# Causal attention with a mixture of experts: row maxima by one masked reduction for each query block and head

## The chip, the cores and the metric

The kernel runs on one core of a Trainium2 chip. The core has five engines that run their own instruction streams and wait for one another by semaphores: TensorE (PE in the profile; its weight loads are listed as PEld), VectorE (DVE), ScalarE (ACT), GpSimd (POOL) and SyncE (SP), which issues transfers. The metric is the time of one execution on the device in microseconds. The kernel before takes 564.23 us, the median of three runs (562.38, 564.23, 564.98).

## The reference

The input x has 8 batches of 512 tokens with 128 features. The result is x plus a causal attention of 16 heads of 8 dimensions and plus a mixture of 8 experts (two for each token, by a softmax over router logits) with one shared expert; both work on the layer-normalised x. Cut to the part that the change touches:

```python
h = jnp.swapaxes((xn @ W1 + b1).reshape(B, S, H, 3 * d), 1, 2)   # H = 16, d = 8, S = 512
q, k, v = h[..., :d], h[..., d:2*d], h[..., 2*d:]
w = jnp.einsum('bhqd,bhkd->bhqk', q, k) / d ** 0.5
mask = jnp.tril(jnp.ones((S, S)))
w = jax.nn.softmax(w * mask - (1.0 - mask) * 1e6, axis=-1)       # causal
a = jnp.einsum('bhqk,bhkd->bhqd', w, v)
...
x + a.reshape(B, S, E) @ Wp + bp + moe(xn)
```

The softmax needs, for each query and head, the largest score over the keys up to the query itself.

## The kernel before

**Tiling.** A batch has four blocks of 128 queries (NC = 4, P = 128). Four heads form a group, so that there are 32 groups (8 batches, 4 groups each), and the loop at line 1219 goes over them. A group's work is cut into five steps (TILES, line 329), 160 steps in all. Two things happen with the scores. The transposed scores (keys on the partitions; tile scT, function fill) go through the exponential on ScalarE (weigh, L465, tile pT) and then into the products with v (attend, L489). Before that the maximum of each query's row has to be known, so the scores are computed a first time with the queries on the partitions (tile sc, function peak_scores) only to take their maxima (function maxima). This runs AHEAD = 9 steps before the exponential of the same scores. At the end of a group, shift_parts turns the maxima of the four heads into two parts, shift transposes them (mT) and put_shift stores them by two small transfers into two extra rows of the queries, so that the later product scT subtracts the maxima by itself.

**Which maxima come from which tile.** Every sc tile has 128 partitions, two heads (index t) and 512 columns of f32, and there is one such buffer (pool m_ps). Of a group's five steps, steps 0 and 2 (MASKED_TILES) hold the four diagonal blocks of two heads each: eight products of 128 columns. Steps 1 and 3 hold, for two heads each, query block 3 with the keys of blocks 0 to 2 (384 columns) and query block 1 with the keys of block 0 (128 columns). Step 4 holds query block 2 with the keys of blocks 0 and 1 for all four heads. Query block 0 has nothing below its diagonal block.

**Masking.** Only diagonal blocks need the mask. In most of the kernel the mask lies in sc before the products are added to it: prepare (called at line 1236, one step ahead) lets ScalarE copy mask_q into the buffer (L371), and the products accumulate onto it (start is false). While the routing still runs, prepare is not called; there peak_scores puts the mask on by four products of an identity with mask_q2 (mask_half, L324).

**Maxima.** Diagonal tiles are reduced into diag by one reduction of 1024 elements (L417), steps 1 and 3 into tops by two reductions (768 elements, L421, and 256, L422), step 4 by one of 1024 (L412). shift_parts first combines tops and diag by a maximum (L427). tops is set to a very small number once (L194), so that block 0, for which nothing is written there, takes its maximum from diag.

**What sets the order.** The order on TensorE, VectorE, ScalarE and SyncE is the program's order, written out by hand (line 87); each engine takes its instructions one after the other, and one that waits holds up all behind it. A step (lines 1222 to 1254) issues, in this order: fill and the exponential (weigh); the sc products and the maxima of nine steps later (look); one piece of the experts' work (extra): products gu (L651), a tanh on ScalarE (L656), two VectorE instructions th and h (L657, L659); then shift_parts, prepare, a piece of the routing, up to two entries of side (mostly the products y, L682), and what was put off (attend, evacuate, divide, turn, join). Products gu, y and most small ones share three buffers of the pool mi_ps. The routing runs on VectorE until it is done, in the first 140 us or so, and prepare and the routed experts start after it.

Of the kernel before, what the change touches and what calls it, by code (L numbers as in the profile page):

```python
# [10 lines left out]
F32 = mybir.dt.float32  # L11
I32 = mybir.dt.int32
BF16 = mybir.dt.bfloat16
F32R = mybir.dt.float32r
AF = mybir.ActivationFunctionType
ALU = mybir.AluOpType
AX = mybir.AxisListType
# [8 lines left out]
P = 128  # L26
B, S, E = 8, 512, 128
H, D = 16, 8
NC = S // P
# [6 lines left out]
AHEAD = 9  # L36
# [22 lines left out]
MASKED = -1e30  # L59
WHOLE = 1.5 * 2.0**23  # L60
LEAST = -3e38
QK = 4 * D
SIDE = 64
# [4 lines left out]
def attn_moe_kernel(  # L68
# [14 lines left out]
    nc = tc.nc  # L83
    const = ctx.enter_context(tc.tile_pool(name="const", bufs=1))
# [43 lines left out]
    for i in range(NV):  # L128
        t = const.tile([P, NC, H, 32], F32, name=f"v_ext{i}")
# [11 lines left out]
    def constant_rows(t, rows):  # L141
# [4 lines left out]
                fills[:rows].unsqueeze(1).to_broadcast([rows, NU * HP * NC, P]),  # L146
            )

    mask_q = const.tile([P, P], BF16, name="mask_q")
    nc.gpsimd.memset(mask_q, 0.0)  # L150
    nc.gpsimd.affine_select(
        out=mask_q, in_=mask_q, pattern=[[-1, P]], compare_op=ALU.is_ge, fill=MASKED,
        base=0, channel_multiplier=1,
    )
    eye_2 = const.tile([P, 2, P], BF16, name="eye_2")
    mask_q2 = const.tile([P, 2, P], BF16, name="mask_q2")
    mask_k2 = const.tile([P, 2, P], BF16, name="mask_k2")
    for m, sign, compare, fill in (
        (mask_q2, 1, ALU.is_ge, MASKED), (mask_k2, -1, ALU.is_ge, MASKED),
        (eye_2, 1, ALU.not_equal, 1.0),  # L160
    ):
        nc.gpsimd.memset(m, 0.0)
        for t in range(2):
            nc.gpsimd.affine_select(
                out=m[ts(t, SIDE)], in_=m[ts(t, SIDE)], pattern=[[sign * SIDE, 2], [-sign, P]],
                compare_op=compare, fill=fill, base=0, channel_multiplier=sign,
            )
    for t in v_ext:
# [9 lines left out]
        out=before, in_=before, pattern=[[1, P]], compare_op=ALU.is_gt, fill=-1.0,  # L178
        base=0, channel_multiplier=-1,
# [7 lines left out]
        out=upto, in_=upto, pattern=[[1, NE], [-1, NE]], compare_op=ALU.is_ge, fill=0.0,  # L187
        base=0, channel_multiplier=0,
# [2 lines left out]


    tops = const.tile([P, 2, 2, NC], F32, name="tops")
    nc.vector.memset(tops, LEAST)  # L194
    diag = const.tile([P, 2, 2, NC], F32, name="diag")

    xnT = const.tile([E, NT * P], F32, name="xnT")

# [2 lines left out]
    for i in range(2):  # L201
        t = const.tile([P, NF, PAIR], F32, name=f"h{i}")
# [6 lines left out]
        own_p, pattern=[[0, 1]], base=0, channel_multiplier=1, allow_small_or_imprecise_dtypes=True  # L209
# [3 lines left out]
        upto_p, pattern=[[1, P]], base=0, channel_multiplier=0, allow_small_or_imprecise_dtypes=True  # L213
# [14 lines left out]
    at = pool("at", 2)  # L228
# [5 lines left out]
    m_ps = pool("m_ps", 1, space=PSUM)  # L234
# [82 lines left out]
    def rows_of(n, jj, rows):  # L317
        u, i, t = n // 2 % NU, n % 2 * 2 + jj // 2, jj % 2
        at_ = slice(SIDE * t, SIDE * t + rows)
        return qs[at_, u, i, :], ks[at_, u, i, :]  # L320

    def mask_half(out_, t, k, mask):

        nc.tensor.matmul(  # L324
            out_, lhsT=eye_2[ts(t, SIDE), k], rhs=mask, start=False, stop=True,
            skip_group_check=True,
        )

    TILES = [("wide", 0), ("wide", 2), ("mixed", 0), ("mixed", 2), ("half", 0)]
    NTILES = len(TILES)  # L330
# [30 lines left out]

    MASKED_TILES = (0, 2)
    ahead = []

    def prepare(n, i):

        ps = m_ps.tile([P, 2, S], F32, name="sc")
        if i in MASKED_TILES:  # L370
            nc.scalar.copy(  # L371
                ps.rearrange("p t (b k) -> p (t b) k", k=P),
                mask_q.unsqueeze(1).to_broadcast([P, 2 * NC, P]),
            )
        ahead.append(ps)

    def peak_scores(n, i):
        ready_ = bool(ahead)
        ps = ahead.pop() if ready_ else m_ps.tile([P, 2, S], F32, name="sc")

        def part(at_, jj, c, key, count, start):
            q, k = rows_of(n, jj, QK + 1 if n else QK)
            nc.tensor.matmul(  # L383
                ps[:, jj % 2, ts(at_, P) if count == 1 else ds(at_ * P, count * P)],
                lhsT=q[:, ts(c, P)], rhs=k[:, key * P : (key + count) * P],
                start=start, stop=True, skip_group_check=True,
            )

        j = i // 2 * 2
        if i == 4:  # L390
            blocks = [(0, 0, 2, 0, 2, True), (2, 2, 2, 0, 2, False)]
        elif i in MASKED_TILES:
            blocks = [(c, j, c, c, 1, not ready_ and c == 0) for c in range(NC)]
        else:
            blocks = [(0, j, 3, 0, 3, True), (3, j, 1, 0, 1, False)]
        for at_, jj, *rest in blocks:
            for t in range(2):
                part(at_, jj + t, *rest)
        if i in MASKED_TILES and not ready_:
            for k in range(2):  # L400
                for t in range(2):
                    mask_half(
                        ps[:, t].rearrange("p (b k) -> p b k", k=P), t, k,
                        mask_q2[ts(t, SIDE), k].unsqueeze(1).to_broadcast([SIDE, NC, P]),
                    )
        return ps

    def maxima(n, i):

        ps = peak_scores(n, i)  # L410
        if i == 4:
            nc.vector.tensor_reduce(  # L412
                tops[:, :, :, 2],
                ps.rearrange("p t (u k) -> p t u k", u=2), AX.X, ALU.max,
            )
        elif i in MASKED_TILES:
            nc.vector.tensor_reduce(  # L417
                diag[:, :, i // 2, :], ps.rearrange("p t (b k) -> p t b k", k=P), AX.X, ALU.max
            )
        else:  # L420
            nc.vector.tensor_reduce(tops[:, :, i // 2, 3], ps[:, :, : 3 * P], AX.X, ALU.max)  # L421
            nc.vector.tensor_reduce(tops[:, :, i // 2, 1], ps[:, :, 3 * P :], AX.X, ALU.max)  # L422

    def shift_parts(n):

        top = at.tile([P, 2, 2 * NC], F32, name="row_max")
        nc.vector.tensor_tensor(  # L427
            top.rearrange("p t (i c) -> p t i c", c=NC), tops, diag, ALU.max
        )
        parts = at.tile([P, 2, 2, 2 * NC], F32R, name="m_parts")  # L430
        hi, lo = parts[:, :, 0], parts[:, :, 1]
        nc.vector.tensor_scalar_mul(hi, top, -1.0)
        nc.vector.scalar_tensor_tensor(lo, top, -1.0, hi.bitcast(F32), ALU.mult, ALU.subtract)
        return parts
# [298 lines left out]
    total_steps = B * NG * NTILES  # L733
# [48 lines left out]
    count = ro.tile([P, PURE + 2 * MIXED], F32, name="count")  # L782
# [368 lines left out]
    done_routing = []  # L1151
# [50 lines left out]
    for b in range(1, B):  # L1202
        at_ = 5 * NG * (b - 1)
# [15 lines left out]
    for n in range(B * NG):  # L1219
        b, g = divmod(n, NG)  # L1220
        waiting = []
        for i, (kind, j) in enumerate(TILES):
            step = n * NTILES + i
            if i == 1 and n % 2 == 1 and (n + 3) // 2 < 2 * B:
                fetch((n + 3) // 2)
            by_pool = step >= BUSY and len(placed) < NB
            spare = step >= total_steps - AHEAD + 1 and step % 2 == 1
            waiting.append((kind, j, weigh(n, kind, j, by_pool, spare)))
            while to_place:
                to_place.pop(0)()  # L1230
            parts_then = look(step + AHEAD) if step + AHEAD < total_steps else lambda: None
            if step not in alone:
                extra()
            parts_then()
            if done_routing and step + AHEAD + 1 < total_steps:
                prepare(*divmod(step + AHEAD + 1, NTILES))
            if step >= routed:
                some_routing()
            side(step, 2)
            for f in late:  # L1240
                f()
            behind(step)
            late = []
            if i == NTILES - 1 and n == B * NG - 1:
                evacuate(n, av, halves[0])
            if i == 1 and g % 2 == 0:
                av = av_ps.tile([P, S], F32, name="av")
            if i in (1, 4) or (i == 3 and n == B * NG - 1):
                late = [partial(attend, n, waiting, av)]
                waiting = []  # L1250
            if len(placed) == NB:
                for _ in range(2):
                    if to_gather and (to_gather[0][1] < kept or through):
                        gather(*to_gather.pop(0))
        if n == B * NG - 1:
            break
        if g % 2 == 1:
            late.append(partial(evacuate, n, av))
            due(step + 3, partial(divide, n))
        if g == NG - 1:  # L1260
            due(step + 4, partial(turn, b))
            due(step + 5, partial(join, b), behind_all)
# [78 lines left out]
```

## Time and profile before

| what | value |
| --- | --- |
| median of three runs | 564.23 us |
| the profiled execution's own time | 565.0 us |
| its span in the profile | 562.8 us |
| mean granted TensorE clock | 0.992 |
| instructions in the span | 12501 |
| L383, sc products: count, busy, mean | 896, 81.9 us, 282 ns |
| L324, mask products into sc from mask_q2: count, busy, mean | 56, 8.8 us, 382 ns |
| L465, exponential: count, busy, mean | 156, 159.9 us, 1025 ns |
| L657 and L659, th and h: count each, busy | 156, 64.9 us and 66.0 us |

Busy time is the union of an engine's instructions. A group's mean is of its instructions' lengths from start to end; the next instruction on the same engine may start before the end of one that it doesn't wait for. Idle time before a group is put down to whatever ended it. The span is that of the instructions in the trace; the execution's own time has a little more around it.

### The profile page before, as it was taken

Reading aid. Unit: us, or ns where it says so; the run is one execution under the profiler, and the core shown is the slowest. Engines: PE = TensorE matmul, PEld = TensorE weight load, DVE = VectorE, ACT = ScalarE, POOL = GpSimd, SP = SyncE. Lnnn points to the kernel's source line nnn. Section 1 sums busy time; section 2 is a strip of 40 time slices with the busy share of each in tenths; the row PEclk is TensorE's granted clock in tenths of the full one; section 3 lists DMA queues with packets and bytes.
Section 4 is the critical chain, followed back from the end, with each engine's and each line's share of the span. In section 5 each row is a group of like instructions: output and inputs, shape, how many; then the busy total and the mean of one; then the engine's idle time right before and its main releaser. Section 6 shows DMA issues by size and latency. Waiting matters only on the chain.

```text
span 562.8 us, 12501 instructions
## 1 busy us (share of the span) xinstructions
PE 530.4 (94%) x4495; PEld 381.8 (68%) x4495; DVE 435.0 (77%) x1057; ACT 354.6 (63%) x567; POOL 261.8 (47%) x442
## 2 busy tenths in 40 slices
PE   4899988889999999999999999999999999989994
PEld 3676655557675777777776777667776777768762
DVE  5878998999877877777786887777787877877731
ACT  4453444463566866777677776677677767766553
POOL 8630020001342656666556656656555755543730
PEclk9999998899999999999999999999999999999999
DMA  7651362616228495685829584775928596750694
GB/s 217 146 75 19 77 116 58 96 59 122 65 64 142 131 154 147 118 204 115 156 72 160 176 137 124 129 168 134 175 84 152 154 155 185 147 135 4 103 255 95
DMA packets 34114, 70.72 MB, mean 126 GB/s; under 512 B 7028, under 2 KB 9336, under 8 KB 34054
## 3 DMA queue, kind: packets, MB, share of 16 engines
q1 hardware_dynamic: 26278, 56.47, 45.7%
q0 software_dynamic: 6912, 13.20, 12.3%
q8 instruction: 36, 0.59, 0.5%
q10 hardware_dynamic: 864, 0.27, 0.2%
q14 instruction: 24, 0.20, 0.2%
HBM read 52.38 MB, written 17.33 MB: 124 GB/s over the span
## 4 chain that ended last, share of the span: by engine, by line
PE 76%; DVE 18%; DMA 2%; ACT 2%; issue 2%; SPq 0%; DVEq 0%; ACTq 0%
PE gu L651 25%; PE av L489 12%; PE y L682 11%; PE scT L339 9%; PE sc L383 9%; DVE diag L417 3%; PE qk_ps L264 3%; DVE there L1065 2%; DMA qs<-mT 2%; DVE tops L421 2%; DVE h L659 1%; DVE th L657 1%; PE s_ps L627 1%; PE p_ps L577 1%; PE ot L540 1%
## 5 line engine op out<-in xcount | busy, mean ns | idle before, releaser
L465 ACT ACTIVATE pT<-scT 128x1024 f32<-128x1024 f32 x156 | 159.9, 1025 | 66.3 <-PE scT L339 28.3
L472 POOL TENSOR_SCALAR_AFFINE_SELECT pT<-pT 128x256 f32<-128x256 f32 (+1 forms) x174 | 73.7, 437 | 186.5 <-ACT pT L465 182.8
L651 PE MATMUL gu<-sT,w 128*128 128x256 f32 (+1 forms) x480 | 122.5, 382 | 0.3 <-DVE h L659 0.3
L417 DVE TENSOR_REDUCE diag<-sc 128x8 f32<-128x1024 f32 x64 | 78.2, 1221 | 45.1 <-PE sc L383 32.4
L656 ACT ACTIVATE th<-gu 128x256 f32<-128x256 f32 x156 | 59.8, 383 | 65.5 <-PE gu L651 61.0
L383 PE MATMUL sc<-ks,qs 33*128 33x128 f32 (+3 forms) x896 | 81.9, 282 | 9.9 <-DVE tops L422 4.2
L651 PEld LDWEIGHTS gu<-sT,w 128*128 128x128 f32 x480 | 76.6, 189 | 17.2 <-DVE h L659 0.5
L489 PE MATMUL av<-pT,v_ext 128*32 128x512 f32 (+3 forms) x1024 | 82.9, 441 | 1.8 <-ACT pT L465 1.3
L657 DVE SCALAR_TENSOR_TENSOR th<-th,gu 128x256 f32<-128x256 f32 x156 | 64.9, 416 | 23.2 <-ACT th L656 19.0
L339 PE MATMUL scT<-qs,ks 35*128 35x512 f32 (+3 forms) x498 | 78.6, 372 | 3.5 <-DMA qs<-mT 2.3
L666 POOL DMA_INDIRECT results<-o,goal x72 | 73.2, 1016 | 16.2 <-issue 16.2
L613 POOL DMA_INDIRECT s<-table,token x72 | 69.9, 971 | 21.0 <-issue 16.7
L339 PEld LDWEIGHTS scT<-qs,ks 35*128 35x128 f32 x498 | 39.6, 184 | 58.7 <-issue 24.9
L383 PEld LDWEIGHTS sc<-ks,qs 33*128 33x128 f32 (+1 forms) x896 | 66.9, 187 | 17.8 <-DVE diag L417 4.9
L659 DVE TENSOR_TENSOR h<-gu,th 128x256 f32<-128x256 f32 x156 | 66.0, 423 | 5.4
L421 DVE TENSOR_REDUCE tops<-sc 128x2 f32<-128x768 f32 x64 | 60.8, 950 | 1.8 <-PE scT L339 0.5
L682 PE MATMUL y<-w,h 128*128 128x128 f32 x432 | 60.0, 275 | 0.7 <-DVE parts L266 0.7
L682 PEld LDWEIGHTS y<-w,h 128*128 128x128 f32 x432 | 57.2, 191 | 4.6 <-DVE parts L266 1.1
L371 ACT CAST sc<-mask_q 128x1024 f32<-128x1024 bf16 x50 | 51.0, 1020 | 6.1 <-DVE tops L422 4.5
L651 PE MATMUL gu<-xnT,ws_sb 128*128 128x256 f32 x192 | 54.1, 408 | 0.0
L489 PEld LDWEIGHTS av<-pT,v_ext 128*32 128x32 f32 x1024 | 25.4, 109 | 24.0 <-issue 14.4
L412 DVE TENSOR_REDUCE tops<-sc 128x4 f32<-128x1024 f32 x32 | 39.0, 1220 | 2.3 <-PE sc L383 2.0
(209 smaller groups left out, 577.5 us busy)
## 6 DMA issues: line engine op xcount, KB each, us to landing
w<-in_w_exp_dram SPq DMA_DIRECT2D x40, 576.0 KB
ks<-dk SPq DMA_DIRECT2D x60, 128.0 KB
dq<-parts SPq DMA_DIRECT2D x16, 256.0 KB
dk<-parts SPq DMA_DIRECT2D x16, 256.0 KB
qs<-dq SPq DMA_DIRECT2D x64, 64.0 KB
x_sb<-results POOLq DMA_DIRECT2D x16, 256.0 KB
qs<-dq SPq DMA_DIRECT2D x30, 128.0 KB
table<-rows SPq DMA_DIRECT2D x4, 520.0 KB
```

The source lines that it names most:

```text
L339: nc.tensor.matmul(out_, lhsT=k[:, ts(i, P)], rhs=q[:, i * P :], start=first, stop=True, skip_group_check=True,)
L383: nc.tensor.matmul(ps[:, jj % 2, ts(at_, P) if count == 1 else ds(at_ * P, count * P)], lhsT=q[:, ts(c, P)], rhs=k[:, key * P : (key + cou ...
L417: nc.vector.tensor_reduce(diag[:, :, i // 2, :], ps.rearrange("p t (b k) -> p t b k", k=P), AX.X, ALU.max)
L421: nc.vector.tensor_reduce(tops[:, :, i // 2, 3], ps[:, :, : 3 * P], AX.X, ALU.max)
L465: nc.scalar.activation(pT, ps, AF.Exp, scale=D**-0.5)
L472: m = nc.gpsimd.affine_select(out=d, in_=d, pattern=[[0, d.shape[1]], [1, P]], compare_op=ALU.is_ge, fill=0.0, base=0, channel_multiplier=-1,)
L489: nc.tensor.matmul(av[32 * jj : 32 * jj + 32, c * P :], lhsT=v_ext[b % NV][:, c, at_, :], rhs=weights, start=(c == 0 and g % 2 == 0), stop ...
L651: nc.tensor.matmul(gu[:, i, part], lhsT=w[c][:, ds(i * FP + f * P, P)], rhs=sT[:, part], start=True, stop=True,)
L657: nc.vector.scalar_tensor_tensor(th, th, 1.0, gu[:, 0], ALU.add, ALU.mult)
L659: nc.vector.tensor_tensor(h[own_, f], gu[own_, 1], th[own_], ALU.mult)
L666: d = nc.gpsimd.indirect_dma_start(results, bass.IndirectOffsetOnAxis(ap=goal[:, at_ : at_ + 1], axis=0), o, None, bounds_check=PLACES - 1 ...
L682: nc.tensor.matmul(y, lhsT=h[:, f, ts(c, P)], rhs=w[c % len(w)][:, ds(2 * FP + f * P, P)], start=(f == 0), stop=(f == NF - 1),)
```

## The change

The scores of a query block and head are no longer split into a diagonal block and the rest. One product covers all keys up to and with the block's own, and one VectorE instruction adds a mask to it and takes the maximum along the row. Steps 0 and 2 of a group now hold query block 3 of two heads (512 columns each), steps 1 and 3 blocks 2 and 0 (384 and 128 columns each), and step 4 block 1 of all four heads (256 columns each). The number of columns in a group stays what it was, 5120; the products of a group become 16 instead of 28. The mask is a strip of 512 columns, until, made once on GpSimd: zero, but MASKED above the diagonal in the last 128 columns. A block of c + 1 key blocks uses its last (c + 1) x 128 columns. The instruction writes the masked scores back to their place in sc and the maximum to one column of tops. With it go prepare and the copies of the mask, the mask products into sc, mask_q and mask_q2, diag, the first setting of tops, and the maximum that combined tops and diag.

```diff
-    mask_q = const.tile([P, P], BF16, name="mask_q")
-    nc.gpsimd.memset(mask_q, 0.0)
-    nc.gpsimd.affine_select(
-        out=mask_q, in_=mask_q, pattern=[[-1, P]], compare_op=ALU.is_ge, fill=MASKED,
-        base=0, channel_multiplier=1,
-    )
...
-    mask_q2 = const.tile([P, 2, P], BF16, name="mask_q2")
     mask_k2 = const.tile([P, 2, P], BF16, name="mask_k2")
     for m, sign, compare, fill in (
-        (mask_q2, 1, ALU.is_ge, MASKED), (mask_k2, -1, ALU.is_ge, MASKED),
+        (mask_k2, -1, ALU.is_ge, MASKED),
         (eye_2, 1, ALU.not_equal, 1.0),
     ):
...
     tops = const.tile([P, 2, 2, NC], F32, name="tops")
-    nc.vector.memset(tops, LEAST)
-    diag = const.tile([P, 2, 2, NC], F32, name="diag")
+    until = const.tile([P, S], BF16, name="until")
+    nc.gpsimd.memset(until, 0.0)
+    nc.gpsimd.affine_select(
+        out=until, in_=until, pattern=[[-1, S]], compare_op=ALU.is_ge, fill=MASKED,
+        base=S - P, channel_multiplier=1,
+    )
...
-    def prepare(n, i):
-        ps = m_ps.tile([P, 2, S], F32, name="sc")
-        if i in MASKED_TILES:
-            nc.scalar.copy(
-                ps.rearrange("p t (b k) -> p (t b) k", k=P),
-                mask_q.unsqueeze(1).to_broadcast([P, 2 * NC, P]),
-            )
-        ahead.append(ps)
...
     def peak_scores(n, i):
-        ready_ = bool(ahead)
-        ps = ahead.pop() if ready_ else m_ps.tile([P, 2, S], F32, name="sc")
...
+        ps = m_ps.tile([P, 2, S], F32, name="sc")
         j = i // 2 * 2
         if i == 4:
-            blocks = [(0, 0, 2, 0, 2, True), (2, 2, 2, 0, 2, False)]
-        elif i in MASKED_TILES:
-            blocks = [(c, j, c, c, 1, not ready_ and c == 0) for c in range(NC)]
+            blocks = [(0, 0, 1), (2, 2, 1)]
+        elif i % 2 == 0:
+            blocks = [(0, j, 3)]
         else:
-            blocks = [(0, j, 3, 0, 3, True), (3, j, 1, 0, 1, False)]
-        for at_, jj, *rest in blocks:
+            blocks = [(0, j, 2), (3, j, 0)]
+        for at_, jj, c in blocks:
             for t in range(2):
-                part(at_, jj + t, *rest)
...
+                q, k = rows_of(n, jj + t, QK + 1 if n else QK)
+                nc.tensor.matmul(
+                    ps[:, t, ds(at_ * P, (c + 1) * P)], lhsT=q[:, ts(c, P)],
+                    rhs=k[:, : (c + 1) * P], start=(at_ == 0), stop=True,
+                    skip_group_check=True,
+                )
+        return ps, blocks

     def maxima(n, i):
-        ps = peak_scores(n, i)
...
+        ps, blocks = peak_scores(n, i)
+        for at_, jj, c in blocks:
+            for t in range(2):
+                cols = slice(at_ * P, (at_ + c + 1) * P)
+                nc.vector.tensor_tensor_reduce(
+                    ps[:, t, cols], ps[:, t, cols], until[:, S - (c + 1) * P :], 1.0, LEAST,
+                    ALU.add, ALU.max, tops[:, t, jj // 2, c : c + 1],
+                )

     def shift_parts(n):
-        top = at.tile([P, 2, 2 * NC], F32, name="row_max")
-        nc.vector.tensor_tensor(
-            top.rearrange("p t (i c) -> p t i c", c=NC), tops, diag, ALU.max
-        )
+        top = tops.rearrange("p t i c -> p t (i c)")
...
             parts_then()
-            if done_routing and step + AHEAD + 1 < total_steps:
-                prepare(*divmod(step + AHEAD + 1, NTILES))
```

## The prediction

> **What bounds the kernel now.** I read first the busy times and the chain of waits, to see which engine sets the end; then busy time by stage; then the groups of instructions with shapes kept apart, for prices; then the timeline, for the distance from one start to the next. The page first (busy time, then the chain by engine):
>
> ```profile
> PE 530.4 (94%) x4495; PEld 381.8 (68%) x4495; DVE 435.0 (77%) x1057; ACT 354.6 (63%) x567; POOL 261.8 (47%) x442
> ...
> PE 76%; DVE 18%; DMA 2%; ACT 2%; issue 2%; SPq 0%; DVEq 0%; ACTq 0%
> ```
>
> TensorE (PE) holds the chain, but VectorE (DVE) owns 18% of it, and ScalarE (ACT), from which the change takes its copies, only 2%. By stage (busy us of each engine, instructions in brackets, then granted clock and DMA share):
>
> ```profile
> 0.00:26.00 26.00, 17.32 (x74) 12.55 (x74) 18.99 (x77) 12.23 (x25) 19.66 (x78) 1.00 0.69 191
> 26.00:142.00 116.00, 106.46 (x943) 70.60 (x945) 104.81 (x286) 55.32 (x86) 13.67 (x37) 0.97 0.40 77
> 142.00:535.00 393.00, 386.88 (x3260) 286.47 (x3253) 303.98 (x674) 274.55 (x441) 223.16 (x323) 1.00 0.63 132
> 535.00:562.80 27.80, 19.73 (x225) 12.14 (x225) 7.19 (x23) 12.47 (x17) 5.34 (x7) 0.96 0.77 175
> ...
> 60.00:140.00 80.00, 71.60 (x701) 46.61 (x697) 75.64 (x220) 39.08 (x53) 5.72 (x11) 0.96 0.44 92
> ```
>
> So there are two regimes. While the routing runs (26 to 142 us) VectorE is nearly full: 75.64 of 80 us, 94.6%, in its densest part, beside a PE at 89.5%. After it (142 to 535) PE is full, 386.88 of 393, 98.4%, and VectorE has 89 us to spare. No peak score (sc) is written before 26 or after 535, so the change acts on the two middle stages. They hold 7 and 25 of the 32 four-head groups, as L412, which runs once per group, starts at 39.0, 55.0, 72.0, 85.5, 104.7, 123.9, 142.3 and so on.
>
> Prices (group, shapes, count | busy, mean ns of one | idle before it, and its releaser):
>
> ```profile
> L417 DVE TENSOR_REDUCE diag<-sc 128x8 f32<-128x1024 f32 x64 | 78.2, 1221 | 45.1 <-PE sc L383 32.4 <-PE sc L324 4.5 <-PE gu L651 4.4
> L421 DVE TENSOR_REDUCE tops<-sc 128x2 f32<-128x768 f32 x64 | 60.8, 950 | 1.8 <-PE scT L339 0.5 <-PE sc L383 0.5
> L412 DVE TENSOR_REDUCE tops<-sc 128x4 f32<-128x1024 f32 x32 | 39.0, 1220 | 2.3 <-PE sc L383 2.0
> L422 DVE TENSOR_REDUCE tops<-sc 128x2 f32<-128x256 f32 x64 | 26.4, 412 | 0.0
> L371 ACT CAST sc<-mask_q 128x1024 f32<-128x1024 bf16 x50 | 51.0, 1020 | 6.1 <-DVE tops L422 4.5 <-DVE tops L412 1.3
> ```
>
> Between 950 and 412 ns lie 512 elements: 1.05 ns per element, and some 145 ns that each instruction pays anyway. The timeline (start, length) tells how much of that is hidden:
>
> ```profile
> 264.19 0.15 DVE L639 TENSOR_TENSOR w_own<-s,second 128x4 f32<-128x4 f32 x1
> 264.38 0.16 DVE L641 TENSOR_TENSOR scale<-w_own 128x2 f32<-128x2 f32 x1
> 264.48 0.96 DVE L421 TENSOR_REDUCE tops<-sc 128x2 f32<-128x768 f32 x1
> 265.35 0.42 DVE L422 TENSOR_REDUCE tops<-sc 128x2 f32<-128x256 f32 x1
> 265.95 0.42 DVE L657 SCALAR_TENSOR_TENSOR th<-th,gu 128x256 f32<-128x256 f32 x1 [0.18 <-ACT th L656]
> 266.40 0.42 DVE L659 TENSOR_TENSOR h<-gu,th 96x256 f32<-96x256 f32 x1
> ```
>
> L422 needs nothing of L421 and starts 0.87 us after it, 0.80 for 768 elements and 0.07. L659 waits for L657's result and starts 0.45 after it, 0.267 for 256 elements and 0.187. The tiny L641 waits for L639 and starts 0.19 after it; L421, which doesn't wait, starts 0.10 after L641 (0.078 at the median of such pairs). So an instruction costs its elements plus 0.07 us where the next is free, plus 0.187 us where the next waits for its end.
>
> **Removed on VectorE.** Each row counted until the next one starts, the means are 1.189 (L417), 0.869 (L421), 0.369 (L422), 1.214 (L412) and 0.166 us (L427, the combining maximum). A group has 2, 2, 2, 1 and 1 of them: 6.23 us.
>
> **Added on VectorE.** A group gets 16 masked reductions: four each of 512, 384, 128 and 256 elements, 5120 as before, 5.33 us at 1.04 ns. In the changed program's instruction list each is a main instruction and a read-out of one element per partition into tops, and every main one after the first of its tile waits on VectorE's own semaphore. Neither has a row here. From below: the next main cannot start before this one has ended, 187 ns a pair over its elements. From above: the read-out waits for the drained main and the next main for the read-out, twice 187, 374 ns. I take the read-out as following free (65 ns) and then costing what the tiny L639 costs a waiter (187): 252 ns, since a one-element write is nearest to that row. A group is then 5.33 + 16 x 0.252 = 9.37 us, or +3.13 (8.33, +2.1, at the low end; 11.32, +5.1, at the high one). Queued behind these waits are th and h (L657, L659); for h wait the y products (L682) and, over the three "mi" buffers, the next gu (L651); for the maxima waits the next sc product, as sc has one buffer.
>
> A rule of the Trainium skill bears on this: VectorE: DVE Perf Modes, section "The DRAIN you can't avoid", has the next op start only when the pipe is empty. The starts of L421 and L422 (0.87 apart, row 0.96) disagree. By the rule whole rows would count on both sides, 5.33 + 16 x (0.145 + 0.151) = 10.07 against 6.55 us for a group, +3.5 instead of +3.13, some 13 us more in the end. The same page, section "Two Vector instructions with no wait between them", counts an op with an accumulator output as two instructions; no run here shows one yet.
>
> **Removed on PE.** From first sc product to the next other product a diagonal tile takes 0.54 us (eight of 128 columns); two products of 512 columns are priced by scT, 0.34:
>
> ```profile
> 260.99 0.61 PE L383 MATMUL sc<-ks,qs 33*128 33x128 f32 x8
> 261.53 1.13 PE L651 MATMUL gu<-sT,w 128*128 128x256 f32 x4
> ...
> 266.54 0.50 PE L339 MATMUL scT<-qs,ks 35*128 35x512 f32 x2
> 266.88 0.41 PE L383 MATMUL sc<-ks,qs 33*128 33x256 f32 x4
> ```
>
> The other tiles keep four products each. That is 0.2 us x 50 tiles = 9.9 us off PE after 142 us. Before it, 14 diagonal tiles with four mask products each (L324, 56 x 382 ns) shrink from 1.04 to 0.34 us, 9.8 us; I count nothing for these, as VectorE decides there (were it not full, PE would hand back up to 9.8).
>
> **Removed on ScalarE, moved, and at no cost.** The 50 copies (51 us) go; ScalarE is 63% busy and 2% of the chain, so I count 0, bounded by a gain of 2%, 11 us. They also held sc for 1.02 us between VectorE's last read and PE's next product; now VectorE alone releases it. No DMA is moved. GpSimd's mask building trades rows of 0.20 + 0.28 + 0.30 + 0.85 us for a memset and a select over 512 columns (L472 takes 0.62 for that many), hidden as its setup ends near 13.5 us and the first sc product starts at 26.1; uncovered it would be 1 us at most.
>
> **The sum.** Early stage: (104.81 + 7 x 3.13) / 0.946 = 133.9 us against 116, +17.9. Late stage: PE would need (386.88 - 9.9) / 0.984 = 383.1; VectorE needs (303.98 + 25 x 3.13) / 0.946 = 404.1 and is the bound, against 393, +11.1. Together +29.0. The profiled run took 565.0 (span 562.8 and 2.2 around it), 0.8 over the median of 564.2, which the three runs' spread covers; on the median I forecast 593.
>
> **Rivals.** (1) *The read-out hides*, 187 to 220 ns a pair. For it: a one-element instruction can be as short as 78 ns to a free follower. At 187 the early stage gives +10.3; VectorE's late need, 376.9, falls below PE's 383.1, -9.9: 564.6. At 220 it is 576. (2) *Faster*: the pair's wait is no wait for the end, so a pair costs 65 + 78 = 143 ns, +1.39 a group. Early +5.1, late -9.9 since PE's shorter diagonal tiles decide: 559.4. It decides below 184 ns, where both stages cancel; against it stands the semaphore wait in the instruction list. (3) *The read-out is serialized*, 374 ns: early +32.4, late (303.98 + 127) / 0.946 = 455.6, +62.6: 659. For it: L659 and L641 show that a dependent start costs 187 every time. (4) *Lockstep*: with PE at 93% (377.0 of 404.1 us) and VectorE at 95%, and one sc buffer between them, neither reaches 94.6%; at the 90.4% of the whole early stage the same work gives 140.2 and 422.9 us, +54: 618. Against it: 60 to 140 us held 94.6% beside a PE at 89.5%.
>
> **Chances and range.** Forecast, pair at 220 to 300 ns (576 to 619): 0.50. Rival 1: 0.15. Rival 2: 0.09. Rivals 3 and 4, above 619: 0.26. A change of under 0.5% (561.4 to 567.0) can't be told from none here. Rival 2 gives faster 0.08; rivals 1 and 2 around zero, same 0.07; the rest slower, 0.85. From 568 to 640 I leave out about 2 in 10: rival 2 with half of rival 1 below, the full price of rival 3 above.
>
> **What would show it.** Right: VectorE above 500 us busy and over 90% between the stages, its share of the chain above half; starts of successive mains of 256 elements about 0.52 us apart; PE idle before sc, released by VectorE; ScalarE near 304 us. Wrong: a pair under 0.46 us at 256 elements with PE still above 97% late (rivals 1, 2), above 0.6 us (3), or VectorE below 92% with PE below 92% (4). An element rate other than 1.04 ns in the main instruction would break the sum at its first term.

## The result and the profile after

The changed kernel takes 582.89 us (median of four runs, 581.5 to 584.8) against 563.31 us for the kernel before beside it: a ratio of 1.032, 95% interval 1.027 to 1.037. It is slower by 19.6 us. The profiled run took 582.0 us with a span of 580.1.

The page of the changed kernel, busy times and the chain by engine:

```profile
PE 535.5 (92%) x4055; PEld 364.8 (63%) x4055; DVE 498.1 (86%) x1824; ACT 309.4 (53%) x517; POOL 261.7 (45%) x439
...
PE 63%; DVE 29%; issue 4%; ACT 2%; POOL 1%; DMA 0%; DVEq 0%; ACTq 0%; POOLq 0%
```

VectorE is busy for 63 us more and its part of the chain grows from 18% to 29%; TensorE keeps the larger part. ScalarE lost 45 us of work, and nothing is to be seen of it in the time. Busy time by stage, in the same columns as before (PE, PEld, DVE, ACT, POOL, granted clock, DMA). The bounds are the same events as 142 and 535 before: the first reduction of step 4 in group 6 and in group 31, now near 157 and 553:

```profile
26.00:157.00 131.00, 113.23 (x814) 72.70 (x816) 120.31 (x449) 55.50 (x86) 14.06 (x38) 0.86 0.36 70
157.00:553.00 396.00, 386.18 (x2957) 268.66 (x2950) 351.53 (x1274) 229.82 (x390) 223.14 (x322) 1.00 0.61 131
```

The stage of the routing grew by 15 us (116 to 131) and the long stage after it by 3 (393 to 396). In the first, VectorE's busy time grew by 15.5 us, as much as the stage itself, and its idle time stayed where it was (11.2 us before, 10.7 now): there VectorE's new work and the added time are of one size. (That is not a rule for the stage: e7_split_inner below adds 7.7 us there and pays 2.) In the second VectorE got 47.5 us more to do and the time hardly moved. The 3 us by themselves are not more than profiles differ: by the same events this stage took 391.5, 395.8 and 396.6 us in three later runs with the same late groups (e5, e11, e12), 390.7 in e2_late_only, and 388.6 in e3_early_only, whose late groups are those of the kernel before. The medians of e2_late_only say it better. PE's granted clock in the routing stage fell from 0.97 to 0.86, a point that comes back below.

The groups with their shapes kept apart (count | busy, mean ns | idle before, releasers), the four lengths of the masked reduction and the read-out:

```profile
L386 DVE CUSTOM_DVE_ANT_0 sc<-sc,until 128x512 f32<-128x512 f32 x128 | 89.2, 697 | 17.3 <-PE sc L373 11.9 <-PE gu L615 1.2 <-POOL rstd L798 0.6
L386 DVE DVE_READ_ACCUMULATOR2_ANT tops<- 128x1 f32 x512 | 71.9, 140 | 0.0
L386 DVE CUSTOM_DVE_ANT_0 sc<-sc,until 128x384 f32<-128x384 f32 x128 | 71.7, 560 | 4.0 <-PE sc L373 0.9 <-issue 0.3
...
L386 DVE CUSTOM_DVE_ANT_0 sc<-sc,until 128x256 f32<-128x256 f32 x128 | 55.0, 430 | 5.5 <-PE sc L373 1.2 <-PE s_ps L591 1.1
...
L386 DVE CUSTOM_DVE_ANT_0 sc<-sc,until 128x128 f32<-128x128 f32 x128 | 38.3, 299 | 4.4
```

The timeline of VectorE over one tile of steps 1 and 3 (start, length) shows what a pair costs:

```profile
274.66 0.54 DVE L386 CUSTOM_DVE_ANT_0 sc<-sc,until 128x384 f32<-128x384 f32 x1
275.14 0.13 DVE L386 DVE_READ_ACCUMULATOR2_ANT tops<- 128x1 f32 x1
275.30 0.57 DVE L386 CUSTOM_DVE_ANT_0 sc<-sc,until 128x384 f32<-128x384 f32 x1
275.78 0.14 DVE L386 DVE_READ_ACCUMULATOR2_ANT tops<- 128x1 f32 x1
275.96 0.30 DVE L386 CUSTOM_DVE_ANT_0 sc<-sc,until 128x128 f32<-128x128 f32 x1
276.18 0.14 DVE L386 DVE_READ_ACCUMULATOR2_ANT tops<- 128x1 f32 x1
276.35 0.30 DVE L386 CUSTOM_DVE_ANT_0 sc<-sc,until 128x128 f32<-128x128 f32 x1
276.57 0.14 DVE L386 DVE_READ_ACCUMULATOR2_ANT tops<- 128x1 f32 x1
276.57 0.42 DVE L621 SCALAR_TENSOR_TENSOR th<-th,gu 128x256 f32<-128x256 f32 x1
```

The read-out starts 83 ns after the main instruction's elements are through (0.48 us after the start for 384 elements, 0.22 for 128, at 1.04 ns each). The next masked reduction, which waits, starts 0.16 to 0.18 us after the read-out, 175 ns at the median of 352. But th, which waits for nothing on VectorE, starts with the read-out. So a pair costs 258 ns over its elements where the next one waits, and 83 where none does, as behind the last of a tile.

Of PE's waits for another engine those for sc are the longest, for its products and for their weight loads (engine, line, waited for: us in total, times, longest), all until the maxima (tops) had been read:

```profile
PEld sc L373 <- DVE tops L386: 31.6, 45, 2.6
PE sc L373 <- DVE tops L386: 18.5, 23, 2.4
```

### The profile page after: what moved, and what is told of

Same layout as the page of the kernel before. It is cut to its first block, busy times and chain, and to the rows that moved or that the text cites. A ratio compares the mean times of both kernels' runs of the same rounds, so it can differ in the third digit from the quotient of the medians.

```text
span 580.1 us, 12319 instructions
## 1 busy us (share of the span) xinstructions
PE 535.5 (92%) x4055; PEld 364.8 (63%) x4055; DVE 498.1 (86%) x1824; ACT 309.4 (53%) x517; POOL 261.7 (45%) x439
## 4 chain that ended last, share of the span: by engine, by line
PE 63%; DVE 29%; issue 4%; ACT 2%; POOL 1%; DMA 0%; DVEq 0%; ACTq 0%; POOLq 0%
PE gu L615 19%; DVE sc L386 14%; PE av L453 11%; PE y L646 9%; PE sc L373 8%; PE scT L336 7%; PE qk_ps L261 3%; DVE h L623 2%; DVE tops L386 2%; DVE th L621 2%; DVE there L1029 1%; DVE parts L263 1%; PE p_ps L541 1%; PE s_ps L591 1%; ACT pT L429 1%
## 5 line engine op out<-in xcount | busy, mean ns | idle before, releaser
L386 DVE CUSTOM_DVE_ANT_0 sc<-sc,until 128x384 f32<-128x384 f32 (+3 forms) x512 | 254.2, 497 | 31.1 <-PE sc L373 13.9
L373 PE MATMUL sc<-ks,qs 33*128 33x384 f32 (+5 forms) x512 | 76.6, 354 | 21.2 <-DVE tops L386 18.5
L453 PE MATMUL av<-pT,v_ext 128*32 128x512 f32 (+3 forms) x1024 | 86.0, 455 | 1.8 <-ACT pT L429 1.3
L386 DVE DVE_READ_ACCUMULATOR2_ANT tops<- 128x1 f32 x512 | 71.9, 140 | 0.0
L373 PEld LDWEIGHTS sc<-ks,qs 33*128 33x128 f32 (+1 forms) x512 | 43.2, 191 | 36.5 <-DVE tops L386 31.6
L615 PE MATMUL gu<-xnT,ws_sb 128*128 128x256 f32 x192 | 58.2, 431 | 0.7 <-DVE h L623 0.5
L615 PEld LDWEIGHTS gu<-xnT,ws_sb 128*128 128x128 f32 x192 | 35.2, 203 | 12.5 <-issue 4.8
L653 ACT ACTIVATE o<-y,scale 128x128 f32<-128x128 f32 x72 | 26.5, 368 | 25.8 <-PE y L646 20.5
```

Of the source, the lines that this page charges most:

```text
L373: nc.tensor.matmul(ps[:, t, ds(at_ * P, (c + 1) * P)], lhsT=q[:, ts(c, P)], rhs=k[:, : (c + 1) * P], start=(at_ == 0), stop=True, skip_gro ...
L386: nc.vector.tensor_tensor_reduce(ps[:, t, cols], ps[:, t, cols], until[:, S - (c + 1) * P :], 1.0, LEAST, ALU.add, ALU.max, tops[:, t, jj ...
L453: nc.tensor.matmul(av[32 * jj : 32 * jj + 32, c * P :], lhsT=v_ext[b % NV][:, c, at_, :], rhs=weights, start=(c == 0 and g % 2 == 0), stop ...
L615: nc.tensor.matmul(gu[:, i, part], lhsT=w[c][:, ds(i * FP + f * P, P)], rhs=sT[:, part], start=True, stop=True,)
```

## The experiments

All ran beside the kernel before on the same chip, whose median there was 559.8 (e1 to e4), 560.4 (e5 to e8), 560.0 (e9 and e10) and 566.1 us (e11 and e12); ratios are to that. Three dots in a diff stand for lines left out.

Three theories were to be told apart. *VectorE*: the loss is the time of the 512 masked reductions, most of it the wait of each for the one before. *Clock*: the loss is PE at half clock in the routing stage, after its work got thinner. *Lockstep*: the one sc buffer makes PE and VectorE wait for each other.

**Plain reductions without the mask (e1_plain).** Merged products stay.

```diff
-                nc.vector.tensor_tensor_reduce(
-                    ps[:, t, cols], ps[:, t, cols], until[:, S - (c + 1) * P :], 1.0, LEAST,
-                    ALU.add, ALU.max, tops[:, t, jj // 2, c : c + 1],
-                )
+        if i == 4:
+            nc.vector.tensor_reduce(
+                tops[:, :, :, 1], ps.rearrange("p t (u k) -> p t u k", u=2), AX.X, ALU.max
+            )
+        else:
+            for at_, jj, c in blocks:
+                nc.vector.tensor_reduce(
+                    tops[:, :, jj // 2, c], ps[:, :, ds(at_ * P, (c + 1) * P)], AX.X, ALU.max
+                )
...
```

> Merged products as in the changed kernel, but the maxima are taken by plain reductions (one of 1024 elements for the steps with block 3 and with block 1, two of 768 and 256 for the others) and no mask is added to them: the row maximum then also covers the up to 127 later keys of the query's own block, a larger shift for the same softmax. VectorE theory (the loss is the 512 masked reductions with their read-outs): VectorE falls to 6.1 us a group, the routing stage is back at 112 to 116 us, the late stage goes to PE's 383 us, total 545 to 555 us. Clock theory (the loss is that PE, given fewer products, lets its clock fall while the routing runs): the half clock and the loss stay, 575 us or more.

Measured 550.01 us, ratio 0.984 (0.979 to 0.990). Its stages, by the same events:

```profile
26.00:138.00 112.00, 99.89 (x802) 64.94 (x799) 103.64 (x280) 54.88 (x85) 13.55 (x37) 0.95 0.43 81
138.00:519.00 381.00, 378.16 (x2953) 268.93 (x2951) 303.29 (x647) 230.12 (x391) 222.63 (x322) 1.00 0.63 136
```

VectorE is back at 103.6 and 303.3 us, the stages at 112 and 381, as the VectorE theory has it. The late stage is now 12 us shorter than before. Most of that is PE's merged products, once VectorE doesn't take it back; e4_before_no_mask below tells them (9 us) from what left with the masks. The half clock shrank to 10 us although PE has no more products here than in the changed kernel, so the thinner products alone don't cause it.

**The change in one stage only (e2_late_only, e3_early_only).** A function new_way(n) picks the path, n >= 7 in the one and n < 7 in the other; 7 is the group at which the kernel before begins to copy the mask ahead.

```diff
+    def new_way(n):
+        return n >= 7
...
     def maxima(n, i):
+        if new_way(n):
+            return maxima_new(n, i)
...
```

> The kernel before for groups 0 to 6 and the changed way for groups 7 to 31. VectorE theory, as the changed kernel's trace has it (late stage +3 us): 563 + 3 = 566 us, 564 to 569, with the routing stage and its clock as before. The term as predicted (+11 us late): 574 us.

> The changed way for groups 0 to 6 and the kernel before for groups 7 to 31. VectorE theory and clock theory both: about +15 us in the routing stage, 578 us, 575 to 581; the two halves add up to the whole change (+19.6). If they don't add up, the stages work on each other. Half clock as in the changed kernel, near 37 us.

Measured: late only 563.19 us, ratio 1.007 (1.004 to 1.009), +3.4 us; early only 576.77 us, 1.034 (1.028 to 1.040), +16.9 us. They add up to 20.3 against the whole change's 19.6. (The first lies just under its range of 564 to 569 in absolute time; the kernel before was 3.5 us faster there, too.) Five sixths of the loss come from the 7 groups that run beside the routing, and the 25 others cost 3 us together. The half clock came with the early part alone (27 us; 14 in the late one), below the 37 that was expected.

**The kernel before without its masks in sc (e4_before_no_mask).** Score products and reductions as before; the copies and, in the lines left out, the 56 mask products of the routing stage are gone.

```diff
     def prepare(n, i):
         ps = m_ps.tile([P, 2, S], F32, name="sc")
-        if i in MASKED_TILES:
-            nc.scalar.copy(
-                ps.rearrange("p t (b k) -> p (t b) k", k=P),
-                mask_q.unsqueeze(1).to_broadcast([P, 2 * NC, P]),
-            )
...
```

> The kernel before with its own products and reductions, but no mask in sc: ScalarE's 50 copies and the 56 mask products are gone, and the maxima also cover the later keys of the query's own block. What the copies were worth was priced at 0, with 11 us as the bound: 552 to 563 us. If ScalarE's copies held up PE's chain: at or below 552. If PE's mask products in the routing stage kept its clock up: the half clock grows from 7 to 20 us or more.

Measured 558.02 us, ratio 0.997 (0.993 to 1.000): 2 us, at the edge of what can be told from nothing. ScalarE's 51 us of copies were hidden, as priced. The half clock rose from 7 to 14 us, under the 20 set for it, so the mask products weren't what kept it up. Between this kernel and e1_plain lie the merged products (and the combining maximum L427, 0.17 us a group), 8 us of the medians, and 9.0 us of the late stage (390.4 and 381.4 from the end of group 6 to that of group 31): the 9.9 of the forecast, nearly.

**Keeping the clock up (e5_warm; later e11_warm_light with one product for three, and e12_warm_alone with four in the twelve steps without experts).**

```diff
     def peak_scores(n, i):
+        if n < 7:
+            warm = misc([P, S], "warm")
+            for _ in range(3):
+                nc.tensor.matmul(warm, lhsT=ones16, rhs=until, start=True, stop=True)
         ps = m_ps.tile([P, 2, S], F32, name="sc")
```

The two later kernels differ from the changed one in a second place, which their expectations don't name: the loop that refines the inverse root of the normalisation on GpSimd runs once in e11_warm_light and four times in e12_warm_alone, in place of three times.

```diff
-        for _ in range(3):
+        for _ in range(1):
             eng.tensor_tensor(a, r, r, ALU.mult)
...
```

So neither is a clean test. GpSimd spends 1.6 and 6.6 us on that loop in place of 5.0, all before 32 us, that is 3.4 us less and 1.6 us more.

> The changed kernel with three products of 512 columns that nobody reads ahead of the sc products of each tile of groups 0 to 6, where PE waits for sc to come free. Clock theory (the routing stage is long because PE, idle while it waits, runs 37 us at half clock): the half clock falls to 10 us or less and the time to 568 to 576 us. VectorE theory: the half clock falls too, but the routing stage stays within 2 us of the changed kernel's 131, total 580 to 586 (or longer, as the products take PE time).

> The changed kernel with one product of 512 columns that nobody reads (0.21 us) ahead of the sc products of each tile of groups 0 to 6, a third of those of the earlier run with three, so that they take at most 7.5 us of PE time in the 131 us of the routing stage, within its idle 18 us. Clock theory: the half clock falls from 37 us to under 20 and the time by 4 to 10 us, to 572 to 579 us. VectorE theory: half clock down, time 580 to 585 as for the changed kernel.

> As the run beside it, but four such products in the twelve steps alone (those of the routing stage that hold no piece of the experts, where PE has least to do), 10 us in all. Clock theory: 572 to 579 us. VectorE theory: 580 to 585 us.

Measured: 582.66 us, ratio 1.043 (1.037 to 1.050); 587.53, 1.039 (1.035 to 1.042); 589.46, 1.042 (1.038 to 1.046). All three lie above the changed kernel's 1.032, and e11 and e12 miss both of their ranges from above (the kernel before was at 566 there). The routing stage of e5_warm, whose first step 4 of group 6 is at 160.6, beside the changed kernel's above:

```profile
26.00:160.00 134.00, 125.15 (x904) 71.24 (x903) 120.10 (x448) 55.44 (x85) 13.99 (x38) 0.97 0.37 68
```

The clock is back at 0.97, VectorE's busy time is the same 120 us, and the stage is 3 us longer, not shorter. The first test was weak, as PE spent 12 us more on products nobody needs; the lighter ones (half clock 24 us in both) were to mend that, and they too gained nothing, e11_warm_light even with less work on GpSimd. Keeping the clock up by such products doesn't pay, and nothing here shows the clock as the cause of the whole loss. That it costs nothing isn't shown: among the runs of one kernel the slower ones have the lower clock (early only: 574.9 us at 0.970, 581.3 at 0.960), and which of the two makes the other was not tried. A comparison at the end of this section puts a number on it.

**A buffer for each head (e6_split_outer, e7_split_inner).** The first goes head after head, the second block after block with the heads within, as the changed kernel does. A masked reduction writes its scores back in place, and the program waits between two that use the same tile; with a tile for each head the waits on the instruction directly before are 6 of a group in the first and none in the second.

```diff
-        ps = m_ps.tile([P, 2, S], F32, name="sc")
+        ps = [m_ps.tile([P, S], F32, tag=f"sc{t}", name="sc") for t in range(2)]
...
-            spare = step >= total_steps - AHEAD + 1 and step % 2 == 1
+            spare = False
```

> The changed kernel with one sc buffer for each head in place of one for two, head after head: PE can refill the first while VectorE reduces the second (lockstep theory), and of the 11 waits of a masked reduction for the one before it in the same buffer 6 are left in a group. The last four odd steps use scT in place of sc. Lockstep theory (PE held up by the one buffer): nearly the whole loss is back, 563 to 568 us, the same as in the next run. VectorE theory (the waits are the price): 5 x 0.175 = 0.9 us less a group, routing stage 6 us shorter, late stage at PE's 383 to 390, total 566 to 576.

> As the run before, but block after block and head within: a masked reduction never waits for the one directly before it. VectorE theory: a pair then costs its elements and 83 ns, a group 6.7 us instead of 8.6; the routing stage loses 3 us against the kernel before instead of 15, total 553 to 566 us, and at least 4 us below the run before. Lockstep theory: no difference to the run before.

Measured: 576.59 us, ratio 1.030 (1.023 to 1.037), and 569.62 us, 1.019 (1.011 to 1.027). Both missed their ranges from above, by a third thing: the stretch after the last group's maxima took 33 and 36 us in place of 24.5, with PE at half clock for 17 and 27 us of it, of which below. Up to there the profiles of the changed kernel, the first and the second run take 555.6, 542.4 and 529.0 us. The second differs from the first only in the order. VectorE's timeline in it:

```profile
274.06 0.60 DVE L386 CUSTOM_DVE_ANT_0 sc<-sc,until 128x384 f32<-128x384 f32 x1
274.58 0.14 DVE L386 DVE_READ_ACCUMULATOR2_ANT tops<- 128x1 f32 x1
274.58 0.33 DVE L386 CUSTOM_DVE_ANT_0 sc<-sc,until 128x128 f32<-128x128 f32 x1
274.82 0.14 DVE L386 DVE_READ_ACCUMULATOR2_ANT tops<- 128x1 f32 x1
274.82 0.33 DVE L386 CUSTOM_DVE_ANT_0 sc<-sc,until 128x128 f32<-128x128 f32 x1
```

The next main instruction now starts together with the read-out of the one before: the 175 ns are gone from all 352 places, and about 16 to 32 ns of each come back as a longer main instruction (0.25 us from start to start for 128 elements, 115 ns over the elements; 83 before). Lockstep expected no difference between these two runs; 7 us of the medians and 13 of the stages speak for the waits, though the two intervals overlap a little. How much of the first run's gain is the second buffer and how much the five waits it lost stays open. Against the changed kernel, the second run has both the second buffer and no waits.

**What the mask costs without a wait (e8_split_plain).** As e7_split_inner, with tensor_reduce on the same 16 pieces.

> As the run before, with plain reductions of the same 16 pieces and no mask added (the maximum also covers the later keys of the query's own block). It tells what adding the mask costs where no wait does. VectorE theory: 16 x 70 ns + 5.33 = 6.45 us a group, within 4 us of the run before. If the masked instruction has a price of its own beyond that (element rate, reading the mask): more than 8 us faster than the run before.

Measured 561.41 us, ratio 0.999 (0.994 to 1.003), 8.2 us under the run before it: at the threshold. On VectorE the masked instruction does have a price of its own: starts of independent plain reductions of 512, 384 and 128 elements lie 608, 465 and 198 ns apart, those of masked ones 616, 498 and 248. Whether that is the read-out, the second operand or the scores written back was not told apart. How much time it costs is less sure: the two profiles differ by 0.3 us in the routing stage, 2.7 in the late one and 2.5 after the last maxima, where no masked reduction runs.

**The last four odd steps again in sc (e9_split_spare), and the plain kernel again (e10_plain_again).**

```diff
+        if spare:
+            ps = [m_ps.tile([P, S], F32, tag=f"sc{t}", name="sc") for t in range(2)]
...
+        if spare:
+            for t in range(2):
+                nc.scalar.activation(pT[:, t], ps[t], AF.Exp, scale=D**-0.5)
```

> The run with a buffer for each head, block after block and head within, with the last four odd steps in sc again (two exponentials of 512 in place of one of 1024). The masks stay and the maxima are exact. In the three split runs the stretch after the last group's maxima was 33 to 36 us against 24.5 in the changed kernel; if that comes from these four steps, 8 to 11 us are back: 558 to 562 us, the kernel before within 1%. If it comes from the split itself: 566 to 572.

> The merged products with plain reductions and no mask in the maxima once more, for a narrower interval on the same chip as the run beside it: ratio 0.980 to 0.990 to the kernel before, 548 to 554 us.

Measured: 560.60 us, ratio 1.000 (0.997 to 1.003), and 549.56 us, 0.979 (0.975 to 0.984). The stretch after the last maxima is 25.2 us again, with 2 us of half clock, so those four steps were the 8 to 11 us. The stages of e9_split_spare by the same events, and below them the routing stage of e7_split_inner:

```profile
26.00:149.60 123.60, 112.75 (x816) 72.74 (x817) 112.78 (x449) 55.53 (x86) 13.93 (x37) 0.88 0.38 74
149.60:532.00 382.40, 380.63 (x2952) 270.80 (x2945) 329.08 (x1273) 230.33 (x390) 222.90 (x322) 1.00 0.62 136
...
26.00:144.40 118.40, 106.54 (x822) 68.36 (x823) 112.47 (x450) 55.29 (x86) 14.01 (x38) 0.94 0.40 77
```

With the same masks and the same exact maxima as the changed kernel, the 3.2% are gone from the total once each head has its buffer and no masked reduction waits for the one before. They are not all gone from where they arose: the routing stage is 7.5 us shorter than the changed kernel's but 7 longer than before (116), and the late stage, at 382 against 393, pays for that with the merged products' gain. In e7_split_inner, whose instructions are the same up to the last steps, the routing stage is 5 us shorter still (118.4), with as much VectorE work and 14 us at half clock in place of 31 (37 in the changed kernel). So of the 13 us by which e7_split_inner shortens the changed kernel's routing stage, some 5 go along with the clock, and whether the clock makes them stays open; the other 7.5 are there in e9_split_spare too, at nearly the changed kernel's clock (0.88 against 0.86). And the plain kernel beats both: 1.6% and 2.1% under the kernel before in two measurements (the second a shade below its range). Its maximum may be that of a later key of the same block of 128. The softmax is the same for any shift, as long as that key's score isn't so far above the row's own that all its exponentials vanish; with other data this has to be looked at again.

## Why the prediction was right, and where it wasn't

**Direction, engine and stage: right.** The routing stage was forecast to pay most, +17.9 us, because VectorE is full there; it paid 15 in the trace and 16.9 alone (e3_early_only). ScalarE's copies were priced at 0 and PE's merged products at 9.9 us late; the runs give 2 and 9.0. The element rate came out too: a read-out starts 616 ns after a main instruction of 512 elements and 217 after one of 128, 1.04 ns for each of the 384 between. In the late stage the engine was wrong: VectorE was to become the bound there and cost 11.1 us, but PE stayed it (97.5% busy), and the change cost 3.

**The pair: right where it waits, too dear where it doesn't.** The forecast gave every one of the 16 pairs of a group 252 ns. The 11 that are followed by a waiting one cost 258. The 5 last of their tiles cost 83, since what follows them on VectorE doesn't wait. A group is then 5.33 + 11 x 0.258 + 5 x 0.083 = 8.59 us against the forecast's 9.37, +2.36 in place of +3.13. On average a pair cost 203 ns, which is not the forecast's band (220 to 300) but that of its first rival.

**The packing: too good.** With the right pair the sum as it was set up would give (104.81 + 7 x 2.36) / 0.946 = 128.2 us early and, VectorE at 383.6, a bound level with PE's 383.1 late: +3 us in all. So the two errors covered each other, and that the time fell well inside the range is in part luck. VectorE's 94.6%, taken from the densest 80 us, was not reached: it is 91.8% in the routing stage and 88.8% late, beside a PE at 97.5% (93.8% and 91.1% with the 34 ns between a read-out's end and the main instruction that waits for it, which count as idle). The fourth rival's mechanism is what the forecast left out in its middle: two nearly full engines that hand one buffer to and fro leave PE waiting for sc, and so the 9 us that PE had saved late did not show. PE's waits in the late stage, in the changed kernel and then in e9_split_spare, whose late stage is 13 us shorter:

```profile
PE sc L373 <- DVE tops L386: 6.0, 10, 1.1
PEld sc L373 <- DVE tops L386: 15.8, 29, 1.4
...
PE sc L377 <- DVE tops L390: 0.9, 4, 0.3
PEld sc L377 <- DVE tops L390: 2.8, 7, 0.6
```

The rival's price, +54 us with the dear pair, was far too high.

**The signs that it set.** Kept: starts of successive mains of 256 elements 0.525 us apart (0.52 forecast), PE idle before sc until VectorE released it, ScalarE at 309 us. Not kept: VectorE at 498 us (above 500) and 89.5% between the stages (above 90), both narrowly, and its share of the chain at 29% (above half), by far. In the routing stage the fourth rival's sign is there, VectorE at 91.8% with PE at 86.4%.

**The other rivals.** The hidden read-out (187 to 220 ns a pair, 564.6 to 576 us) has the mean pair right, 203 ns, and the time wrong, for the same missing packing. The faster case had the right condition: without the waits the pair falls below the 184 ns from which it was to decide (115 ns in e7_split_inner), and the loss indeed vanishes (e9_split_spare at 1.000), though no gain comes of it (0.997 to 1.003). A serialized read-out, 374 ns, is excluded by the timeline.

**The rule set against the trace.** The section that the prediction cites from the Trainium skill (VectorE: DVE Perf Modes, section "The DRAIN you can't avoid") goes on to say that a next op which is not held starts earlier. L421 and L422 agree with that, and so does e7_split_inner, where a main instruction of 0.33 us is followed by the next after 0.25. So the prediction's "disagree" and its +3.5 a group rest on half of what the page says; its sum doesn't use them.

**Not foreseen**: the granted clock of 0.86 in the routing stage. The trace showed how full PE was, but the forecast didn't ask what its longer waits would do to its clock.

## What to carry to other kernels

A fused instruction that replaces two engines' work by one is priced by what follows it: here the elements were the same, and the loss was gone from the total once a buffer for each head took away one wait after each of 352 instructions, in the order that the changed kernel already had. Look for the stage in which the receiving engine is full and price its new work there; an average share of 77% hid a stage at 90%, and 95% in its densest part. And ask whether the exact value is needed at all: an upper bound of the row maximum was cheaper than either exact way.

## What the runs showed of the hardware

- A masked reduction is two rows in the trace, the main instruction and a read-out of 140 ns for one element per partition. A next instruction that needs neither starts with the read-out; one that waits starts 175 ns after that.
- PE's granted clock fell to half in pieces of 3.4, 6.8 and 10.2 us in the changed kernel's routing stage, after idle times shorter than these. Before one of the two longest pieces, PE's row reads (start, length, what it waited for):

```profile
106.98 0.79 PE L373 MATMUL sc<-ks,qs 33*128 33x384 f32 x4 [2.39 <-DVE tops L386]
```

PE idled from 104.6 to 107.0 us and the half clock ran from 105.8 to 116.0; other pieces followed gaps of 0.9 to 1.6 us. In the 3.4 us ahead of each of the six pieces PE was idle for 1.1 to 1.9 us. Not every such gap is followed by one: 1.2 us at 56.6 here and 1.5 us at 108.5 in the kernel before were not. The Trainium skill (TensorE: Matmul & The Clock Gate, section "Part 1: The HAM clock gate") has the clock drop after an idle window of about 3.4 us. The length of the pieces agrees with such a window; the gaps, at most 2.4 us, are shorter than it, so in this kernel a stretch of that length that is only partly idle was enough.
- Products that nobody reads do bring the clock back (0.86 to 0.97 in e5_warm), and no time with it here (134 us for that stage against 131).
